# Background steps spaced by range width in a four-layer graph network

## Chip, cores and metric

The kernel runs on one core of one Trainium2 chip. The metric is the device time of a whole execution in microseconds (us), lower being better. Every engine (PE the matrix engine, PEld its weight loads, DVE the vector engine, ACT the scalar engine, POOL, and SP, which here only issues transfers) works through an instruction stream of its own, and transfers run on queues that SP, ACT and POOL issue to.

## What is computed

A network of 2708 nodes with 512 features and a sparse weighted adjacency matrix `adj` of 2708 x 2708 is run through four layers. Each adds its result to its input and normalizes the rows. Cut to what matters:

```python
deg = maximum((adj != 0).sum(-1), 1)
x = layernorm(x + L0(x, adj))   # (adj + normalized mask) @ x over row sums
x = layernorm(x + L1(x, adj))   # attention, gates, two products with adj
x = layernorm(x + L2(x, adj))   # x@w0 + A x@w1 + A A x@w2 + A A A x@w3
x = layernorm(x + L3(x, adj))   # (adj/deg-normalized @ x + x) @ W + b, relu

# in L1
s_left, s_right = h @ a_left, h @ a_right                  # h = x @ W_sa
e    = where(adj != 0, exp(-leaky_relu(s_left[:, None] + s_right[None, :])), 0)
x_a  = (e / (e.sum(1) + 1e-5)) @ h
x_b  = adj @ (x @ W_gcnb) + b_gcnb
out  = sigmoid(gate_a * x_a + gate_b * x_b)

# in L3
dinv = rsqrt(deg);  a_norm = dinv * (adj + I) * dinv
```

The counts `deg` of layer 3, one for each row of `adj`, are gathered while layer 1 runs: the sign of each element of the transposed matrix is squared (1 where it isn't zero), the squares are added up, and a matmul with ones sums over partitions.

## The kernel before

The matrix is held transposed and split into quarters (11, 12, 21, 22) of 1354 x 1354. Products with it are done in seven partial products instead of eight (P1 to P7; on PE the lines 462, 471, 480, 486, in later stages 1369), for which DVE forms combinations of quarters (s1 to s4, L407).

**Order.** The kernel is not written in the order in which it runs. Each small piece of work is put into a list with a position, `at(pos, fn)`; the list is sorted by position and the pieces are called in that order. The scheduler of the framework then orders the instructions of each engine by that order and its own estimate of times, so an instruction may be placed ahead of others that stand before it in the list. One listed as held, `at(pos, fn, True)`, may not be placed ahead of the instruction before it in the list on its own engine. A unit of position is one of the seven products of one range of columns. Stages start at the positions `S = [0, 28, 35, 91, 119, 147, 175]` and `SB = 63`.

**Stage S[1]** (position 28 to 35, one range of 330 columns) does the adjacency product of layer 1 for the columns from 1024. Beside the products, `comb` forms the sums and stores them in DRAM (SD, shown as As). `score` multiplies fetched rows of x with four vectors (L907), `scores_end` adds the halves into `s_left` and `s_right`, and `score_rows` turns columns of `s_left` into rows in DRAM: `to_rows`, a transpose on PE (L924), a copy on ACT (L926), a store by POOL (L927). `extra1` counts: `pair` has Sign twice and Square on ACT into a bf16 tile `sg` (L973, L974), and an add on DVE into `dg` (L980); `end` has the matmuls with ones (`ds`, L993) and small DVE operations, and `rows` the transpose of the reciprocals. `done1` takes the finished half results C and W through the gates (`pg`, L1018) and the dense product `ps_d` with the weights w (L610), then stores XB.

**Stage S[2]** (position 35 to 63) does the attention product of layer 1 in four ranges of seven positions each, with the columns and widths

```python
RANGES = [(0, 384), (384, 384), (768, 256), (1024, 330)]
RANGES_B = [(512, 256), (0, 256)]
```

Before a tile is used, `prep2` makes the attention weights (ACT L1156 and L1157, DVE L1158); row sums run along (L770). When a half of a range is done, DVE adds its partial results (L523: names C, W, U, P1c), at 5.05 and 7.02 positions into the range, and `done2` has the dense product with it, from 5.15 and 7.12 on.

**Background steps.** Through S[2], 22 steps run beside the product, eleven for each of two sets of 512 columns: ten full ones and a rest. A full step loads four tiles of 128 x 512, one of each quarter, in two halves (`back_load`, POOL L1067). `tally` turns two tiles into squared signs (ACT L1083, L1084) and adds them to the counts `dg` (DVE L1086), twice a step. `back_sums` forms four combinations in place (DVE L1107) and stores each (POOL L1108, As<-bk). The tiles `bk` are six in rotation: four share memory with the weights w, two with xT. `back_end` sums the counts with matmuls (L1115), and `back_rows` makes rows of them, 1.4 to 1.7 positions into the rest step. The tiles `sg` and `dg` share six slots ("nat") with fetched rows and results.

The later stages (SB, S[3] to S[6]) read the stored combinations and, in the last, the counts.

Of the kernel before, what the change touches and what calls it, by code (L numbers as in the profile page):

```python
# [24 lines left out]
ALU = mybir.AluOpType  # L25
P = 128
EPS = 1e-5
NH = 1354
KT = 11
RANGES = [(0, 384), (384, 384), (768, 256), (1024, 330)]  # L30
# [24 lines left out]
KA = 2 * KR - 32  # L55
# [16 lines left out]
def gnn_kernel(ctx: ExitStack, tc: tile.TileContext, x, adjT, w_sa, a_sa, w_gcn, b_gcn, wab, bab, w_hop, w_out,  # L72
               b_out, out):
    nc = tc.nc
# [104 lines left out]
    def at(pos, fn, hold=False):  # L179

        def go():
            n = len(nc.cur_bb.bb.instructions)
            fn()
            held.update(range(n, len(nc.cur_bb.bb.instructions)))

        events.append((pos, len(events), go if hold else fn))
# [500 lines left out]
    S = [0.0, 28.0, 35.0, 91.0, 119.0, 147.0, 175.0]  # L687
# [233 lines left out]
    def to_rows(cols, m, dst):  # L921

        ps = bank("ps_r", [P, P])
        nc.tensor.transpose(ps[:m], cols, ident)  # L924
        t = small.tile([P, P], F32, name="rows", bufs=2)
        nc.scalar.copy(t[:m], ps[:m])  # L926
        nc.gpsimd.dma_start(out=dst, in_=t[:m])  # L927

    def score_rows(R0, h, ts):
        q = slice(h * KT + ts[0], h * KT + ts[-1] + 1)  # L930
        to_rows(s_left[:, q], len(ts), SROW[R0, h])
# [13 lines left out]
    i = 0  # L945
    for R0, n in RANGES:
        full = R0 == RANGES_A[0][0]
        for h in (1, 0):
            ts = tiles_of(R0, n)
            for k in ts:  # L950
                p = S[1] + 0.55 + 0.21 * i
                at(p, lambda t=h * KT + k: get_x1(t))
                at(p + 0.25, lambda t=h * KT + k, w=wt(k), js=range(4 if full else 2): score(t, w, got1, js))
                i += 1
            at(p + 0.26, lambda a=(h * KT + ts[0], len(ts), False): scores_end(*a))
            if full:
                at(p + 0.26, lambda a=(h * KT + ts[0], len(ts), True): scores_end(*a))
            at(p + 1.5, lambda R0=R0, h=h, ts=ts: score_rows(R0, h, ts), True)
    at(p + 0.27, scores_over)
    for i, (h, k) in enumerate((h, k) for g in (4, 0) for h in (0, 1) for k in range(g, g + 4)):  # L960
        p = S[2] + 1.6 + 1.3 * i
# [5 lines left out]
    def extra1(pb, r, R0, n, A):  # L967
        ts = tiles_of(R0, n)

        def pair(keys, w=P):  # L970
            m = pool.tile([P, 2, D], BF, name="sg", tag="nat", bufs=6)
            for h, key in enumerate(keys):
                nc.scalar.activation(m[:w, h, :n], A[(r,) + key][:w, :n], AF.Sign)  # L973
            nc.scalar.activation(m[:w, :, :n], m[:w, :, :n], AF.Square)  # L974
            if R0 not in deg:
                deg[R0] = d = pool.tile([P, 2, D], BF, name="dg", tag="nat", bufs=6)
                nc.vector.tensor_copy(d[:w, :, :n], m[:w, :, :n])
            else:
                d = deg[R0]
                nc.vector.tensor_tensor(d[:w, :, :n], d[:w, :, :n], m[:w, :, :n], ALU.add)  # L980

        for k in range(KW):
            at(pb + 0.1 + 0.8 * k / KT, lambda k=k: pair((("11", k), ("21", k))), True)
            at(pb + 3.9 + 0.8 * k / KT, lambda k=k: pair((("12", k), ("22", k))), True)
        for key, w in (("r", KA), ("r32", 32)):
            at(pb + 4.8, lambda key=key, w=w: pair(((key, 0), (key, 1)), w), True)

        def end(h):
            d = deg[R0]
            ps = bank("ds", [P, 4])  # L990
            for i, q in enumerate(ts):
                wq = wt(q)
                nc.tensor.matmul(ps[:wq, i : i + 1], d[:, h, q * P - R0 : q * P - R0 + wq], ones_bf[:, 0:1], start=True,  # L993
                                 stop=True)
            for i, q in enumerate(ts):
                wq = wt(q)
                o = rdeg[:wq, h * KT + q : h * KT + q + 1]
                nc.vector.tensor_scalar(o, ps[:wq, i : i + 1], 1.0, None, ALU.max)
                nc.vector.tensor_scalar(diag[:wq, h, q : q + 1], o, 1.0, None, ALU.add)
                nc.vector.reciprocal(o, o)  # L1000

        def rows(h):
            to_rows(rdeg[:, h * KT + ts[0] : h * KT + ts[-1] + 1], len(ts),
                    DROW[h][0, ts[0] * P : (ts[-1] + 1) * P].rearrange("(k i) -> k i", i=P))

        at(pb + 5.2, lambda: end(1))
        at(pb + 5.9, lambda: rows(1))
        at(pb + 5.2, lambda: end(0))
        at(pb + 5.9, lambda: rows(0))

    def done1(p0, dp, last, R0, n, h, C, tiles):
        Z = {}
# [35 lines left out]
    back = {}  # L1048
# [13 lines left out]
    def back_load(i0, k, half):  # L1062
        if not half:
            back["next"] = {}
        for hi, hj in QUARTERS[2:] if half else QUARTERS[:2]:
            j0, c0 = hj * NH + k * P, hi * NH + i0
            nc.gpsimd.dma_start(out=back_tile((hi, hj)), in_=adjT[j0 : j0 + P, c0 : c0 + D])  # L1067
        if half:
            back["t"] = back["next"]

    def back_rest_load(i0):
        back["next"] = {}
        for h in range(2):
            a = adjT[:, h * NH + i0 : h * NH + i0 + D]
            rows_over(nc.gpsimd, back_tile((h, 0)), (a[NH - KR : NH], a[2 * NH - KR :]))
            nc.gpsimd.dma_start(out=back_tile((h, 1))[:32], in_=a[2 * NH - 32 :])
        back["t"] = back["next"]

    def tally(pair, w):

        m = pool.tile([P, 2, D], BF, name="sg", tag="nat", bufs=6)
        for h in range(2):
            nc.scalar.activation(m[:w, h, :], pair[h][:w], AF.Sign)  # L1083
        nc.scalar.activation(m[:w], m[:w], AF.Square)  # L1084
        d = back["d"][back["i0"]]
        nc.vector.tensor_tensor(d[:w], d[:w], m[:w], ALU.add)  # L1086

    def back_start(i0):
        back["i0"] = i0
        back.setdefault("d", {})[i0] = pool.tile([P, 2, D], BF, name="dg", tag="nat", bufs=6)  # L1090
        nc.gpsimd.memset(back["d"][i0], 0.0)

    def back_tally():
        t = back["t"]
        for j in range(2):
            tally([t[h, j] for h in range(2)], P)

    def back_rest_tally():
        t = back["t"]
        for j, w in ((0, KA), (1, 32)):  # L1100
            tally([t[h, j] for h in range(2)], w)

    def back_sums(i0, k):
        a21, a22, a11, a12 = (back["t"][q] for q in QUARTERS)
        for m, o, a, b, op in (("s1", a22, a21, a22, ALU.add), ("s3", a21, a11, a21, ALU.subtract),
                               ("s2", a11, a22, a11, ALU.subtract), ("s4", a12, a12, a11, ALU.subtract)):
            nc.vector.tensor_tensor(o, a, b, op)  # L1107
            nc.gpsimd.dma_start(out=SD[m][k * P : (k + 1) * P, i0 : i0 + D], in_=o)  # L1108

    def back_end(i0):  # L1110
        d = back["d"].pop(i0)
        ps = bank("ds", [P, 8])
        for h in range(2):
            for i in range(4):
                nc.tensor.matmul(ps[:, 4 * h + i : 4 * h + i + 1], d[:, h, i * P : (i + 1) * P], ones_bf[:, 0:1], start=True,  # L1115
                                 stop=True)
        for h in range(2):
            q = slice(h * KT + i0 // P, h * KT + i0 // P + 4)
            o = rdeg[:, q]
            nc.vector.tensor_scalar(o, ps[:, 4 * h : 4 * h + 4], 1.0, None, ALU.max)  # L1120
            nc.vector.tensor_scalar(diag[:, h, i0 // P : i0 // P + 4], o, 1.0, None, ALU.add)
            nc.vector.reciprocal(o, o)

    def back_rows(i0, h):
        q = h * KT + i0 // P
        to_rows(rdeg[:, q : q + 4], 4, DROW[h][0, i0 : i0 + D].rearrange("(k i) -> k i", i=P))

    p = S[2] + 1.6
    for i0, _ in RANGES_B:
        at(p, lambda i0=i0: back_start(i0))  # L1130
        for k in range(KW):
            at(p - 0.55, lambda i0=i0, k=k: back_load(i0, k, 0))
            at(p + 0.02, lambda i0=i0, k=k: back_load(i0, k, 1))
            at(p + 0.6, back_tally, True)
            at(p + 0.7, lambda i0=i0, k=k: back_sums(i0, k), True)
            p += 1.12
        at(p, lambda i0=i0: back_rest_load(i0))
        at(p + 0.6, back_rest_tally, True)
        at(p + 1.4, lambda i0=i0: back_end(i0), True)
        at(p + 1.7, lambda i0=i0: back_rows(i0, 0), True)  # L1140
        at(p + 1.72, lambda i0=i0: back_rows(i0, 1), True)
        p += 1.12

    def start2b():
        W[2] = [spare_part(s, g) for s in ("T1", "T2", "T3", "T4") for g in "BD"]
# [597 lines left out]
    for n, i in enumerate(list(nc.cur_bb.bb.instructions)):  # L1743
        p = last if n < 3 * strict else done if n in held else {}
# [44 lines left out]
```

## Time and profile before

| | |
|---|---|
| time, median of 3 runs (lowest to highest) | 2913.36 us (2912.59 to 2916.22) |
| the profiled execution: its time, its span | 2914.74 us, 2913.0 us |
| mean granted TensorE clock | 0.992 |
| S[2], first matmul to first matmul of SB | 554.2 to 1013.7 us |
| busy in S[2]: PE, DVE, ACT, POOL | 436.6, 322.9, 272.7, 124.5 us |
| a bk load of 256 KB, issue to landing (median) | 4.7 us |
| a store As<-bk of 256 KB, issue to landing (median) | 3.6 us |
| Sign, Square of the tally (median) | 614 ns, 1042 ns |
| add of the tally, combination of a step (median) | 692 ns, 686 ns |

The span runs from the first to the last recorded instruction. A line of the timeline gives start, duration, engine, line, operation, output and inputs, shape and count; a bracket at its end is the time for which the engine sat idle before it and whose event ended that. A line of waits gives the engine and line that waited, the one waited for, the total, how often, and the longest. Ends of matmuls are modelled, so a PE that is busy may still be slow: the pace of equal matmuls is what to compare.

### The profile page before, as it was taken

The page shows a single profiled execution, that of the slowest core. Times are in us where ns is not written, and L with a number is a line of the kernel's source. Part 1 is how long each engine was busy: PE and PEld are TensorE (multiplying, and loading weights), DVE is VectorE, ACT ScalarE, POOL GpSimd, SP SyncE. Part 2 cuts the span into 40 slices and gives each one's busy share as a digit, 9 for nine tenths or more (in the row PEclk, how much of TensorE's full clock was granted, in tenths as well). Part 3 has the DMA queues.
Part 4 walks back from the last instruction along what each step waited for, and adds up shares of the span by engine and source line. Part 5 has one row for each costly group of instructions (what it writes and reads, how often), then busy time and mean ns, then how long its engine had stood idle before and what let it go on. Part 6 is the DMA issues. An engine that isn't in the chain of part 4 may idle for free.

```text
span 2913.0 us, 38876 instructions
## 1 busy us (share of the span) xinstructions
PE 2824.2 (97%) x11159; PEld 1909.6 (66%) x11159; DVE 2293.2 (79%) x5890; ACT 662.2 (23%) x1314; POOL 650.6 (22%) x1175
## 2 busy tenths in 40 slices
PE   7999998999999999999999999999999999999998
PEld 5655665556676678787666666666666666656664
DVE  6989688687767667577599787887878878899986
ACT  4554204765557311202200000000000100100001
POOL 0123233212232210213203133030330212501102
PEclk9999999999999999999999999999999999999999
DMA  8666466466666565577667768566675665854642
GB/s 236 199 201 187 136 198 211 133 202 187 192 207 207 167 180 150 182 218 247 218 195 236 215 188 251 168 198 203 193 245 171 180 202 169 256 144 143 181 138 79
DMA packets 404959, 554.41 MB, mean 190 GB/s; under 512 B 68752, under 2 KB 350556, under 8 KB 404744
## 3 DMA queue, kind: packets, MB, share of 16 engines
q1 hardware_dynamic: 330976, 391.33, 45.7%
q0 software_dynamic: 56032, 148.83, 15.5%
q10 hardware_dynamic: 17736, 11.76, 1.4%
q8 instruction: 89, 1.46, 0.2%
q14 instruction: 126, 1.03, 0.1%
HBM read 468.02 MB, written 83.65 MB: 189 GB/s over the span
## 4 chain that ended last, share of the span: by engine, by line
PE 75%; DVE 10%; issue 5%; DMA 5%; POOL 2%; ACT 1%; SPq 1%; POOLq 0%; ACTq 0%; DVEq 0%
PE accd L1369 14%; PE accu L1369 13%; PE accc L1369 13%; PE ps_d L610 7%; PE acca L1369 6%; PE accu L462 4%; PE accd L462 4%; PE accr L1440 3%; PE accc L462 3%; PE acca L462 3%; DMA bk<-in_adjT 2%; DMA As<-bk 1%; DVE z L1314 1%; PE accr L1444 1%; PE ps L649 1%
## 5 line engine op out<-in xcount | busy, mean ns | idle before, releaser
L1314 DVE TENSOR_TENSOR z<-z 128x339 f32<-128x339 f32 (+2 forms) x1176 | 538.4, 490 | 19.9 <-PE accu L1369 10.6
L1387 ACT COPY q<-accu 128x339 f32<-128x339 f32 (+2 forms) x105 | 41.7, 429 | 1057.7 <-PE accu L1369 907.7
L1369 PE MATMUL accc<-s,t 128*128 128x339 f32 (+2 forms) x784 | 233.5, 439 | 0.2 <-DVE s L1314 0.2
L1369 PE MATMUL accu<-z,t 128*128 128x339 f32 (+2 forms) x784 | 227.7, 436 | 4.2 <-DVE z L1314 3.0
L1369 PE MATMUL accd<-z,t 128*128 128x339 f32 (+2 forms) x784 | 227.8, 436 | 2.2 <-DVE q L1451 1.4
L1369 PE MATMUL accc<-z,t 128*128 128x339 f32 (+2 forms) x784 | 226.8, 436 | 0.5 <-ACT q L1387 0.5
L564 POOL TENSOR_TENSOR rstd<-rstd,neg_half 128x1 f32<-128x1 f32 (+3 forms) x91 | 60.2, 662 | 710.0 <-DVE rstd L563 454.5
L1369 PEld LDWEIGHTS accu<-z,t 128*128 128x128 f32 x784 | 148.1, 190 | 70.1 <-DVE z L1314 6.1
L1369 PEld LDWEIGHTS accc<-s,t 128*128 128x128 f32 x784 | 146.8, 190 | 70.7 <-issue 10.2
L1369 PEld LDWEIGHTS accd<-z,t 128*128 128x128 f32 x784 | 148.1, 190 | 67.2 <-DVE q L1451 2.3
L1369 PEld LDWEIGHTS accc<-z,t 128*128 128x128 f32 x784 | 148.2, 190 | 64.8 <-ACT q L1387 1.0
L1393 DVE TENSOR_TENSOR q<-q,accd 128x338 f32<-128x338 f32 (+2 forms) x140 | 67.9, 485 | 148.7 <-PE accd L1369 148.3
L1314 DVE TENSOR_TENSOR s<-z 128x339 f32<-128x339 f32 (+2 forms) x392 | 178.1, 489 | 7.2 <-PE accc L1369 3.1
L1588 POOL DMA_DIRECT2D Y<-y x192 | 104.8, 552 | 327.0 <-DVE y L1583 289.8
L407 DVE TENSOR_TENSOR a<-a,a 128x384 f32<-128x384 f32 (+2 forms) x240 | 118.5, 514 | 7.1 <-ACT sg L973 6.1
L1158 DVE SCALAR_TENSOR_TENSOR a<-a,e 128x384 f32<-128x384 f32 (+2 forms) x160 | 78.4, 507 | 36.2 <-ACT e L1157 34.7
L1156 ACT ACTIVATE e<-row,s_right 128x384 f32<-128x384 f32 (+5 forms) x176 | 95.4, 566 | 37.6 <-DVE a L1158 17.9
L569 ACT ACTIVATE ld<-ld,rstd 128x512 f32<-128x512 f32 (+3 forms) x45 | 36.5, 813 | 263.9 <-DVE rstd L566 98.4
L1451 DVE TENSOR_TENSOR q<-q,accr 128x338 f32<-128x338 f32 (+2 forms) x160 | 69.1, 484 | 22.8 <-PE accr L1444 22.7
L1393 DVE TENSOR_TENSOR q<-q,accu 128x338 f32<-128x338 f32 (+2 forms) x175 | 79.2, 485 | 3.9 <-ACT q L1387 2.7
L1157 ACT ACTIVATE e<-e 128x384 f32<-128x384 f32 (+5 forms) x176 | 80.0, 476 | 1.7
L774 DVE SCALAR_TENSOR_TENSOR s<-a,row 128x384 f32<-128x384 f32 (+2 forms) x152 | 75.3, 508 | 6.0 <-ACT row L759 6.0
(699 smaller groups left out, 5897.6 us busy)
## 6 DMA issues: line engine op xcount, KB each, us to landing
z<-As SPq DMA_DIRECT2D x320, 169.5 KB
z<-As SPq DMA_DIRECT2D x320, 169.0 KB
z<-in_adjT SPq DMA_DIRECT2D x240, 169.5 KB
z<-in_adjT SPq DMA_DIRECT2D x240, 169.0 KB
a<-in_adjT SPq DMA_DIRECT2D x160, 192.0 KB
bk<-in_adjT POOLq DMA_DIRECT2D x80, 256.0 KB, 4.7
As<-bk POOLq DMA_DIRECT2D x80, 256.0 KB, 3.6
z<-As SPq DMA_DIRECT2D x160, 128.0 KB
```

Of the source, the lines that this page charges most:

```text
L407: nc.vector.tensor_tensor(A[r, dst, k][:, :n], A[r, a, k][:, :n], A[r, b, k][:, :n], op)
L462: nc.tensor.matmul(B[home, c][:, :n], X[STAT[p], k][:, c * P : (c + 1) * P], A[r, MOV[p], k][:, :n], start=bool(start and k == k0), stop=k ...
L610: nc.tensor.matmul(o, lhs(c), r, start=c == 0 and n == 0, stop=c == DC - 1, skip_group_check=True)
L774: nc.vector.scalar_tensor_tensor(t[:w, :n], a[:w, :n], 0.0, row[R0, h][:w, :n], ALU.is_gt, ALU.mult)
L1156: nc.scalar.activation(e[:w, :n], row[R0, h][:w, :n], AF.Prelu, bias=s_right[:w, t : t + 1], alpha=0.01)
L1157: nc.scalar.activation(e[:w, :n], e[:w, :n], AF.Exp, scale=-1.0)
L1158: nc.vector.scalar_tensor_tensor(a[:w, :n], a[:w, :n], 0.0, e[:w, :n], ALU.not_equal, ALU.mult)
L1314: nc.vector.tensor_tensor(d[:, :n], Z[x + (k,)][:, :n], Z[y + (k,)][:, :n], op)
L1369: nc.tensor.matmul(B[home][:, :n], stat(v, k), a[:, :n], start=bool(start and k == 0), stop=k == nk - 1, skip_group_check=True)
L1393: nc.vector.tensor_tensor(d[:, :n], s_[:, :n], B[home][:, :n], ALU.add)
L1440: nc.tensor.matmul(ps[r][:, :n], XA[:KA, c * P : (c + 1) * P], R[h, s][:KA, :n], start=True, stop=False, skip_group_check=True)
L1588: nc.gpsimd.dma_start(out=rows[:, :, f * P : (f + 1) * P], in_=o[32 * f : 32 * (f + 1), : m * P].rearrange("p (b d) -> p b d", d=P))
```

## The change

Three groups of edits; no operation of the arithmetic is added, dropped or changed.

1. The background steps get positions from a time scale. A range of n columns counts as n + 60 per position, `place_at` turns a time on that scale into a position, and 22 steps lie at equal distances `dt`. Before, a step took 1.12 positions in every range.
2. `pair` and `tally` only square, and the add is a piece of its own (`add`, `back_add`), listed later: 0.1 position in S[1], 0.08 of a step in S[2]. A step's two tallies are listed apart, too. The squares of the rests in S[1] go from 4.8 to 5.0.
3. `score_rows` is listed at 4.5 (columns from 0) or 6.2 positions into S[1], where each stood 1.5 after its last tile's fetch. In S[1] `end` goes from 5.2 to 7.0 and `rows` from 5.9 to 7.5, both held now.

```diff
-            at(p + 1.5, lambda R0=R0, h=h, ts=ts: score_rows(R0, h, ts), True)
+            at(S[1] + (6.2 if R0 else 4.5) + 0.01 * i, lambda R0=R0, h=h, ts=ts: score_rows(R0, h, ts), True)
...
             nc.scalar.activation(m[:w, :, :n], m[:w, :, :n], AF.Square)
+            ms.append((m, w))
+
+        def add():
+            m, w = ms.pop(0)
             if R0 not in deg:
...
             at(pb + 0.1 + 0.8 * k / KT, lambda k=k: pair((("11", k), ("21", k))), True)
+            at(pb + 0.2 + 0.8 * k / KT, add, True)
             at(pb + 3.9 + 0.8 * k / KT, lambda k=k: pair((("12", k), ("22", k))), True)
+            at(pb + 4.0 + 0.8 * k / KT, add, True)
         for key, w in (("r", KA), ("r32", 32)):
-            at(pb + 4.8, lambda key=key, w=w: pair(((key, 0), (key, 1)), w), True)
+            at(pb + 5.0, lambda key=key, w=w: pair(((key, 0), (key, 1)), w), True)
+            at(pb + 5.0, add, True)
...
-        at(pb + 5.2, lambda: end(1))
-        at(pb + 5.9, lambda: rows(1))
-        at(pb + 5.2, lambda: end(0))
-        at(pb + 5.9, lambda: rows(0))
+        for h in (1, 0):
+            at(pb + 7.0, lambda h=h: end(h), True)
+            at(pb + 7.5, lambda h=h: rows(h), True)
...
         nc.scalar.activation(m[:w], m[:w], AF.Square)
+        back["m"].append((m, w))
+
+    def back_add():
         d = back["d"][back["i0"]]
-        nc.vector.tensor_tensor(d[:w], d[:w], m[:w], ALU.add)
+        for m, w in back["m"]:
+            nc.vector.tensor_tensor(d[:w], d[:w], m[:w], ALU.add)
+        back["m"].clear()
...
-    p = S[2] + 1.6
+    widths = [n + 60 for _, n in RANGES]
+    ends = [7 * sum(widths[:i]) for i in range(5)]
+
+    def place_at(t):
+
+        i = max(i for i in range(4) if ends[i] <= t)
+        return S[2] + 7 * i + (t - ends[i]) / widths[i]
+
+    t0, dt = 1.0 * widths[0], (26.4 / 28 * ends[4] - widths[0]) / 21
+    at_t = lambda j, fn, hold=False: at(place_at(t0 + dt * j), fn, hold)
+    j = 0
     for i0, _ in RANGES_B:
-        at(p, lambda i0=i0: back_start(i0))
+        at_t(j, lambda i0=i0: back_start(i0))
         for k in range(KW):
-            at(p - 0.55, lambda i0=i0, k=k: back_load(i0, k, 0))
-            at(p + 0.02, lambda i0=i0, k=k: back_load(i0, k, 1))
-            at(p + 0.6, back_tally, True)
-            at(p + 0.7, lambda i0=i0, k=k: back_sums(i0, k), True)
-            p += 1.12
-        at(p, lambda i0=i0: back_rest_load(i0))
-        at(p + 0.6, back_rest_tally, True)
-        at(p + 1.4, lambda i0=i0: back_end(i0), True)
-        at(p + 1.7, lambda i0=i0: back_rows(i0, 0), True)
-        at(p + 1.72, lambda i0=i0: back_rows(i0, 1), True)
-        p += 1.12
+            at_t(j - 0.5, lambda i0=i0, k=k: back_load(i0, k, 0))
+            at_t(j + 0.02, lambda i0=i0, k=k: back_load(i0, k, 1))
+            for e in range(2):
+                at_t(j + 0.5 + 0.08 * e, lambda e=e: back_tally(e), True)
+                at_t(j + 0.58 + 0.08 * e, back_add, True)
+            at_t(j + 0.67, lambda i0=i0, k=k: back_sums(i0, k), True)
+            j += 1
+        at_t(j, lambda i0=i0: back_rest_load(i0))
+        for e in range(2):
+            at_t(j + 0.5 + 0.08 * e, lambda e=e: back_rest_tally(e), True)
+            at_t(j + 0.58 + 0.08 * e, back_add, True)
+        at_t(j + 1.3, lambda i0=i0: back_end(i0), True)
+        at_t(j + 1.6, lambda i0=i0: back_rows(i0, 0), True)
+        at_t(j + 1.62, lambda i0=i0: back_rows(i0, 1), True)
+        j += 1
```

More of the change, by code (lines that the diff above doesn't have):

```diff
@@ L968, in extra1 @@
         ts = tiles_of(R0, n)
+        ms = []
         def pair(keys, w=P):
@@ L1084, in tally, with back_tally, back_rest_tally @@
         nc.scalar.activation(m[:w], m[:w], AF.Square)
+        back["m"].append((m, w))
+    def back_add():
         d = back["d"][back["i0"]]
-        nc.vector.tensor_tensor(d[:w], d[:w], m[:w], ALU.add)
+        for m, w in back["m"]:
+            nc.vector.tensor_tensor(d[:w], d[:w], m[:w], ALU.add)
+        back["m"].clear()
     def back_start(i0):
         back["i0"] = i0
+        back["m"] = []
         back.setdefault("d", {})[i0] = pool.tile([P, 2, D], BF, name="dg", tag="nat", bufs=6)
         nc.gpsimd.memset(back["d"][i0], 0.0)
-    def back_tally():
+    def back_tally(j):
         t = back["t"]
-        for j in range(2):
-            tally([t[h, j] for h in range(2)], P)
-    def back_rest_tally():
+        tally([t[h, j] for h in range(2)], P)
+    def back_rest_tally(j):
         t = back["t"]
-        for j, w in ((0, KA), (1, 32)):
-            tally([t[h, j] for h in range(2)], w)
+        tally([t[h, j] for h in range(2)], (KA, 32)[j])
     def back_sums(i0, k):
```

## The prediction

> **What bounds the kernel now.** I read the page's first parts, then busy time by stretch, then the PE timeline for its gaps, then what the engines behind each gap waited for. The page's busy table and its chain of work:
>
> ```profile
> PE 2824.2 (97%) x11159; PEld 1909.6 (66%) x11159; DVE 2293.2 (79%) x5890; ACT 662.2 (23%) x1314; POOL 650.6 (22%) x1175
> ...
> PE 75%; DVE 10%; issue 5%; DMA 5%; POOL 2%; ACT 1%; SPq 1%; POOLq 0%; ACTq 0%; DVEq 0%
> ```
>
> PE is the bound, so a change that leaves the matmuls alone, as this one does, can save only PE gaps and the slow matmuls after them. It touches the end of S[1] and S[2]. I split S[2] at the first matmul of each range (554.2, 678.3, 800.2, 894.2, end 1013.7 us). Columns: stretch; its length; busy PE, PEld, DVE, ACT, POOL; clock; DMA share; GB/s.
>
> ```profile
> 554.20:678.30 124.10, 121.27 (x411) 71.92 (x410) 92.24 (x216) 84.43 (x152) 26.94 (x49) 1.00 0.60 181
> 678.30:800.20 121.90, 119.97 (x422) 76.23 (x421) 83.30 (x215) 70.44 (x137) 32.50 (x60) 1.00 0.61 189
> 800.20:894.20 94.00, 86.79 (x411) 74.27 (x410) 60.65 (x173) 55.89 (x114) 29.34 (x55) 0.96 0.65 207
> 894.20:1013.70 119.50, 108.58 (x428) 76.33 (x426) 86.74 (x227) 61.95 (x120) 35.76 (x65) 0.96 0.60 186
> ```
>
> No other engine is full. PE idles 22.9 us in all, 18 of them in the last two stretches. In the PE timeline it is five gaps (bracket: idle before, and releaser), each at the end of a range where the dense product takes a finished half result (C or P1c, an add of L523):
>
> ```profile
> 640.34 0.70 PE L610 MATMUL ps_d<-T1B,C 128*128 128x256 f32 x2 [2.83 <-DVE C L523]
> 762.17 0.70 PE L610 MATMUL ps_d<-T1B,C 128*128 128x256 f32 x2 [1.93 <-DVE C L523]
> 867.01 1.22 PE L610 MATMUL ps_d<-T1B,C 128*128 128x256 f32 x2 [7.07 <-DVE C L523]
> 902.48 1.19 PE L610 MATMUL ps_d<-T1B,P1c 128*128 128x256 f32 x2 [5.89 <-DVE P1c L523]
> 975.34 1.22 PE L610 MATMUL ps_d<-T1B,C 128*128 128x256 f32 x2 [5.03 <-DVE C L523]
> ```
>
> The matmuls after the three long gaps are slow: the same 16 matmuls of 256 columns take 3.45 us in the chain at 769.76 but 5.62 (867.01 to 872.63), 5.10 (902.48) and 6.22 us (975.34), so 2.17 + 1.65 + 2.77 us more, and 0.27 us after each short gap. The gaps cost S[2] 22.75 + 7.13 = **29.9 us**.
>
> What made DVE late, from the waits of the stretch of S[2] (total us, times, longest):
>
> ```profile
> ACT sg L1083 <- DMA bk<-in_adjT: 65.9, 15, 12.8
> POOL bk L1067 <- DMA As<-bk: 59.1, 36, 4.3
> DVE dg L1086 <- ACT sg L1084: 58.9, 18, 15.2
> ```
>
> This is the background work in a ring of six bk tiles: a load waits for an earlier store, Sign waits for the load, the add of the counts waits for Square, and everything behind that add on DVE waits too. A step that is behind restarts after about 15.5 us (Sign of successive steps at 813.11, 828.56, 843.92, 855.25, 873.14, 888.66). Its list asks for one each 1.12 positions: 19.7 us in ranges 0 and 1 (1.12/7 x 123), **15.0 us in range 2**, 19.1 in range 3. Range 2 asks for more than the ring gives, and there the backlog and the long gaps start.
>
> S[1] ends otherwise. Two PE gaps, both by list order:
>
> ```profile
> 474.23 0.27 PE L924 MATMUL ps_r<-ident,s_left 128*3 128x128 f32 x1 [4.36 <-DVE s_left L918]
> 521.20 0.40 PE L993 MATMUL ds<-ones_bf,dg 128*128 128x1 bf16 x6 [6.29 <-DVE dg L980]
> 518.68 0.49 DVE L523 TENSOR_TENSOR W<-W,accu 128x330 f32<-128x330 f32 x1
> ```
>
> DVE is nearly full there (24.3 of the 25 us from 497 to 522). The last operand of the gate matmuls, W, is written at 519.1.
>
> **What the Trainium skill says.** "TensorE: Matmul & The Clock Gate", Part 1, What's actually happening: after an idle window of about 3.4 us the array runs at half rate, until about 3.4 us of work. The trace agrees: slow matmuls follow the gaps of 5 to 7 us, hardly those of 1.9 and 2.8. "PSUM — Partial Sum Buffer", Engine vs sequencer instructions: the queues of ScalarE, VectorE and GpSimdE are strict FIFO. Agreed: DVE stood 15.16 us before one add at 700.77. "DMA: Bandwidth & Descriptors", Anatomy of one DMA — SWDGE path: 2.0 us plus bytes/436e3, an estimate of 2.6 us for 256 KB. The trace has 4.7 us for a bk load and 3.6 for a store; I use those.
>
> **The change, part by part.** No arithmetic is added or removed. All 22 steps keep 4 loads and 4 stores (bar the two rests), 6 ACT instructions (4 x 0.62 + 2 x 1.04 = 4.6 us), and on DVE 2 adds (0.69) and 4 combinations (0.69), 4.1 us. Only places move.
>
> *Spacing.* With widths 444, 444, 316, 390 and 7 positions each, dt is 479.8, so a step is 1.08 positions in ranges 0 and 1, 1.52 in range 2, 1.23 in range 3. Times the measured lengths that is 19.2, 18.8, 20.4 and 21.0 us: above the ring's 15.5 everywhere. Tallies that fall in each range go from 5, 6, 6, 5 to 6, 6, 5, 5. On POOL the loads and stores move with the step, past stores of XB only; the first loads can't start before 571.6, when the last product with w ends and frees their tiles. By gap:
> - 867: step 15 was listed at 19.0 to 19.1, on top of C (19.05); now 19.27 to 19.53, behind it. Ahead of C vanish 4.1 us of DVE work, waits of 1.21 and 0.42, and the 3.39 us at 846. That is 9.1 against 7.07: gap 0.5 us left, no slow matmuls.
> - 902: P1c is listed at 21.02. Step 16's combinations go from 20.22 to 21.04 and its second add to 21.03: 3.4 us of DVE work falls behind P1c. 5.89 - 3.4 = 2.5, plus 0.3 slow.
> - 975: the rest goes from 25.72 to 26.98, behind C (26.05), and takes 1.37 us of adds and waits of 1.35 and 1.43 along. But step 20 comes to 25.75 to 25.96, with its own 4.1 us. About even: 4.0 plus 1.5.
> - 640: step 3 comes to 4.78 to 4.97, right ahead of C (5.05), where step 2 stood at 4.44. It starts earlier too, so I take a gap of 4.0 plus 0.3, one us more.
> - 762: step 9 at 11.27 to 11.45 for step 8 at 11.16 to 11.26, 3 us later, C at 12.05: 2.5 plus 0.3.
>
> Sum 15.9 us for 29.9: **14.0 saved**.
>
> *Adds after squares.* In S[2] an add now stands 0.08 of a step (1.5 us) after its tally, less than the 2.3 us of Sign, Sign, Square; it hides some of the short waits, none of the long ones, and these are counted above. Each sg tile lives a little longer in the six nat slots; sg and its add still alternate, so I take 0, from -2 to +2. In S[1] the adds didn't wait for Square at all (the trace lists no idle time of L980), so 0 too; the sg tiles there live about one us longer beside the fetched rows. The squares of the rests go from 4.8 to 5.0, with their adds; W (5.06) stays behind them in the list, though the trace has the adds after W (519.89, 520.65), so 0.
>
> *Score rows and sums later.* The first score rows leave 2.5 for 4.5, so the 474 gap (4.36 + 1.69 of slow matmuls) goes, and ds leaves 5.2 for 7.0. But the next thing that PE asks of DVE is W at 519.1, and DVE does the same work up to it. PE only arrives earlier and waits longer. What is left is 521.2 + 0.33 (the ds matmuls) - 519.1 = 2.4, less 0.4 for a longer cold start: **2.0 saved**. Bounds: -14.7 if PE finds other matmuls to do (both gaps with their slow matmuls), +5 if dg, now held until 7.0, leaves y too few nat slots. The rows are due by 5.4 for the row load; 0.85 positions (some 9 us) cover transpose 0.27, copy 0.25 and store 2.2.
>
> *Tail.* Last sums at 27.96, rows at 28.34: PE waits there for adds listed 0.8 positions (12 us) earlier. If that cover is gone, one gap of some 5 us.
>
> Sum -16.0. The profiled execution took 2914.74 us (span 2913.0), 1.38 above the median of 2913.36. 2914.74 - 16.0 - 1.38 = **2897.4**.
>
> **Rivals.** *A: nearly all gaps close* (adds reach DVE in time): four fifths of 29.9, plus 6 of S[1], is -30: 2883. For it: PE is covered wherever DVE isn't late. Against: three blocks now stand right before a result that PE wants. *B: nothing measurable*, 2913: DVE owes the same work at the same results, and gaps only move between ranges. Against: DVE was idle 59 us before adds. *C: slower.* Steps 3, 16 and 20 now stand on the results at 5.05, 21.02 and 26.05. If Square ends later than the result's last matmul, DVE stands at the held add, with the combinations after it, and C comes behind both: up to 4.6 + 2.75 = 7.4 us, plus 2 of cold matmuls. Three of those are 28.2 against 18.4 at these places now, and if 867 keeps its gap nothing pays for it: +9.8, 2923. It decides once ACT is more than some 3 us behind at those places, as it was in 8 of the 18 waits. *D: the steps aren't equally far apart on the chip*, since the scheduler orders engines by its own estimate: gains half as large, 2905.
>
> **How the numbers follow.** About 0.2%, 5.8 us, is what a measurement of this kernel can tell from no change. Main forecast 0.38, A 0.12, D 0.10, B 0.12, C 0.28. Of the three gaining cases (0.60) I put 0.01 within the bound and 0.02 beyond it: faster 0.57, same 0.13, slower 0.30. Range 2879 to 2925: A with most of S[1]'s bound below, C with 2 us of slots above. The faster cases' own range is 2879 to 2907.
>
> **What would show it.** Right: no gap over 2 us at the C of range 2, no wait of Sign for bk over 6 us there, range 2 at 85 to 88 us, the wait of dg for Square under 40 us in all, no PE wait on s_left at 474, the gate matmuls waiting for W instead. Wrong: range 0 longer than 127 us, a wait of over 7 us before the products of ranges 0 or 3, or PE waiting on y or nat slots from 522 to 554. Any gain outside 405 to 1014 us would be another cause.

## The result, and the profile after

The changed kernel took 2931.84 us (median; 2928.94 to 2936.07) against 2913.84 for the kernel before, timed beside it: a ratio of 1.0062, 95% interval 1.0044 to 1.0079, so **18 us slower**, with 2897 forecast. Run again later, in a group of its own, it came to 1.0041 (1.0026 to 1.0057), 12 us slower. The first part of its page and the head of its chain of work:

```profile
PE 2835.4 (97%) x11159; PEld 1919.3 (65%) x11159; DVE 2296.9 (78%) x5890; ACT 660.9 (23%) x1313; POOL 651.9 (22%) x1175
...
PE 76%; DVE 10%; DMA 6%; issue 3%; ACT 2%; POOL 1%; SPq 1%; DVEq 0%; POOLq 0%; ACTq 0%
```

Nothing shows here: every engine has the work of before, and PE is still the bound. The busy times by range (the same columns as before, split at the first matmul of each range) show where it went:

```profile
552.20:685.66 133.46, 123.43 (x417) 73.56 (x415) 97.89 (x239) 91.03 (x166) 33.93 (x63) 0.96 0.59 183
685.66:811.21 125.55, 121.59 (x430) 77.57 (x429) 87.10 (x225) 69.94 (x139) 34.63 (x64) 0.99 0.58 174
811.21:904.23 93.02, 89.12 (x403) 76.00 (x403) 58.29 (x171) 52.15 (x112) 25.79 (x49) 0.94 0.64 206
904.23:1021.27 117.04, 105.89 (x397) 74.35 (x396) 81.09 (x193) 59.82 (x110) 27.80 (x51) 0.94 0.57 170
```

Range 0 went from 124.1 to 133.5 us with 10 us of idle PE in it, range 1 from 121.9 to 125.6, and ranges 2 and 3 together gained only 3.4. The PE timeline has these gaps now, the first in S[1]:

```profile
515.46 2.07 PE L1026 MATMUL pg<-C,wab_pad 128*32 128x330 f32 x4 [6.35 <-DVE C L523]
645.85 1.22 PE L610 MATMUL ps_d<-T1B,C 128*128 128x256 f32 x2 [10.03 <-DVE C L523]
771.58 0.70 PE L610 MATMUL ps_d<-T1B,C 128*128 128x256 f32 x2 [3.96 <-DVE C L523]
872.18 0.98 PE L783 MATMUL rs<-ones_f,run 128*128 128x1 f32 x4 [3.38 <-DVE run L770]
877.30 1.19 PE L610 MATMUL ps_d<-T1B,C 128*128 128x256 f32 x2 [0.52 <-DVE rd L1195]
910.39 1.19 PE L610 MATMUL ps_d<-T1B,P1c 128*128 128x256 f32 x2 [3.83 <-ACT e L1182]
984.30 1.22 PE L610 MATMUL ps_d<-T1B,C 128*128 128x256 f32 x2 [4.78 <-DVE C L523]
1017.79 0.68 PE L599 MATMUL ps_t<-ident,ld 128*128 128x128 f32 x4 [2.54 <-ACT ld L569]
1029.67 0.48 PE L599 MATMUL ps_t<-ident,ld 74*128 74x74 f32 x4 [2.40 <-ACT ld L569]
```

In S[1] both gaps of before are gone, and PE waits for C at the gates. The 7.07 us at C of range 2 has become a wait for row sums, the 2.83 of range 0 has become 10.03, and the last two lines are new: transposes of normalized rows around the start of SB, which PE never waited for before.

The surest measure is the lag: the start of a matmul of the product, changed kernel minus kernel before, the same matmul by count. (The profiled executions took 2934.22 and 2914.74 us; the other run of the changed kernel 2937.13.)

| up to | before, us | lag | lag, run again |
|---|---|---|---|
| S[1], ahead of the score rows | 469.4 | +3.6 | +5.0 |
| S[1], after them | 489.7 | -2.8 | -1.4 |
| range 0, ahead of C | 637.0 | -1.7 | +0.5 |
| range 0, after C | 669.6 | +7.4 | +11.6 |
| range 1, after C | 784.2 | +11.1 | +16.6 |
| range 2, after C | 896.1 | +10.0 | +16.0 |
| range 2, after P1c | 919.5 | +9.2 | +12.4 |
| range 3, after C | 1003.9 | +7.6 | +11.7 |
| SB | 1044.9 | +17.7 | +21.6 |
| last product | 2809.0 | +19.4 | +22.4 |

Two places lose some 10 us each, C of range 0 and the end of S[2], and C of range 1 loses some 4; S[1] gains 6.4 at the score rows. The totals of the ring's waits in S[2] didn't move (before: 65.9, 59.1 and 58.9):

```profile
ACT sg L1091 <- DMA bk<-in_adjT: 66.3, 16, 12.3
POOL bk L1075 <- DMA As<-bk: 62.4, 40, 4.0
DVE dg L1098 <- ACT sg L1092: 59.5, 26, 16.9
```

### The profile page after: what moved, and what is told of

It reads as the page before. It is cut to its first block, busy times and chain, and to the rows that moved or that the text cites. A ratio compares the mean times of both kernels' runs of the same rounds, so it can differ in the third digit from the quotient of the medians.

```text
span 2932.4 us, 38866 instructions
## 1 busy us (share of the span) xinstructions
PE 2835.4 (97%) x11159; PEld 1919.3 (65%) x11159; DVE 2296.9 (78%) x5890; ACT 660.9 (23%) x1313; POOL 651.9 (22%) x1175
## 4 chain that ended last, share of the span: by engine, by line
PE 76%; DVE 10%; DMA 6%; issue 3%; ACT 2%; POOL 1%; SPq 1%; DVEq 0%; POOLq 0%; ACTq 0%
PE accd L1395 13%; PE accu L1395 13%; PE accc L1395 13%; PE ps_d L610 7%; PE acca L1395 6%; PE accu L462 5%; PE accd L462 4%; PE accc L462 4%; PE accr L1466 3%; PE acca L462 3%; DMA bk<-in_adjT 1%; DVE z L1340 1%; PE accr L1470 1%; PE ps L649 1%; DVE vy L907 1%
```

## The experiments

Eleven runs, each timed beside the kernel before on its chip. There the kernel before had medians of 2918 to 2920 us, so the absolute figures in the expectations, which start from 2914, are to be read against that; I use ratios. Lags by place are of one execution each. In e3, e7 and e8 below, whose S[2] is that of the kernel before, the lag still changes by up to 3.4 us at C of range 0 and by up to 2.4 at the other places, but by less than 0.1 from range 3 to SB. A change by place of under about 3 us is therefore not told from none, unless several runs repeat it.

**The change in three parts.** e1, spacing alone, each add in one piece with its square:

```diff
-        back["m"].append((m, w))
+        d = back["d"][back["i0"]]
+        nc.vector.tensor_tensor(d[:w], d[:w], m[:w], ALU.add)
...
-                at_t(j + 0.58 + 0.08 * e, back_add, True)
```

(Diffs in this part are against the changed kernel, unless another is named. Here S[1] is that of the kernel before, too.)

> Only the new time scale of the background steps in S[2]; every add stays in one piece with its square, and S[1] is as before. Theory 1 (the places do it: step 3 and step 9 now stand on DVE right ahead of C of ranges 0 and 1, and the rest step comes behind U in range 3): the whole loss is here, 2926 to 2934 us against 2914, with a gap of 8 to 10 us before the products with C of range 0, about 4 at range 1, under 1 at range 2 (867), and SB starting some 10 us later than C of range 3 explains. Theory 2 (the split of square and add does it, by longer use of the nat slots): within 4 us of the kernel before, or faster by up to 10, since the gaps of range 2 close and no slot is held longer.

Measured: 1.0002 (0.9992 to 1.0011), no difference. The gap in range 0 is there (10.36 us, a lag of 10.3 from that place), and 4.0 more are lost at P1c of range 0; but ranges 2 and 3 pay for it, with 3.9 us at C of range 2, 4.2 at P1c and 8.1 at C of range 3. The end of S[2] loses only 1.5. Theory 1 had the place right and the total wrong. Theory 2 had the total right, but not the whole of its reason: the gaps of range 2 did shrink, and range 0 paid for it.

e2, the split alone, with the old places:

```diff
-        i = max(i for i in range(4) if ends[i] <= t)
-        return S[2] + 7 * i + (t - ends[i]) / widths[i]
+        return S[2] + t
...
-    t0, dt = 1.0 * widths[0], (26.4 / 28 * ends[4] - widths[0]) / 21
+    t0, dt = 1.6, 1.12
```

> Only the split of tally and add in S[2] with the adds 0.08 of a step later; the steps keep 1.12 positions in every range, S[1] is as before. Theory 1 (the places do it): within 3 us of the kernel before (2911 to 2917), no gap over 4 us before C of range 0, the five gaps of before still there. Theory 2 (slots held by squares whose add comes later): 2922 to 2930, with fetches of X rows on SP that wait for an add into dg, and late transposes ps_t before SB.

Measured: 0.9996 (0.9987 to 1.0005). Later adds alone cost nothing, and the gaps of before are there (9.67 at C of range 2, 6.28 at range 3), but for that at C of range 0, which is gone.

e3, the edits of S[1] alone (against the kernel before; the adds as in the change):

```diff
-            at(p + 1.5, lambda R0=R0, h=h, ts=ts: score_rows(R0, h, ts), True)
+            at(S[1] + (6.2 if R0 else 4.5) + 0.01 * i, lambda R0=R0, h=h, ts=ts: score_rows(R0, h, ts), True)
...
+            at(pb + 7.0, lambda h=h: end(h), True)
+            at(pb + 7.5, lambda h=h: rows(h), True)
```

> Only the edits of S[1]: counts added later, score rows at 4.5 and 6.2, sums at 7.0, their rows at 7.5; S[2] is as before. Theory 1: 2 us faster (2910 to 2914); the PE gap before the transposes of s_left (474) is gone, the products with the gates wait for C or W some 4 to 6 us instead, and the loss of 3.7 us at 461 seen in the changed kernel (a matrix load on ACT's queue behind the store of X) does not come back, being a matter of that execution. Rival: the loss at 461 belongs to the edits, and the kernel is 1 to 4 us slower than before.

Measured: 0.9974 (0.9963 to 0.9986), **7.5 us faster**, not 2. The 3.6 us that the changed kernel had lost ahead of the score rows didn't come back. Some 3 us are lost there in some executions (e5 2.7 with the edits, e10 3.0 without) and under 0.4 in others (e3, e4, e6), so they aren't the edits'.

So three parts of +0.5, -1.4 and -7.5 us make +12 to +18 together. Something exists only in the combination. The two next runs look for it.

e10, spacing and split together, with the S[1] of the kernel before:

```diff
-            at(S[1] + (6.2 if R0 else 4.5) + 0.01 * i, lambda R0=R0, h=h, ts=ts: score_rows(R0, h, ts), True)
+            at(p + 1.5, lambda R0=R0, h=h, ts=ts: score_rows(R0, h, ts), True)
...
-            at(pb + 7.0, lambda h=h: end(h), True)
+        at(pb + 5.2, lambda: end(1))
```

> The changed kernel with S[1] as it was before: spacing and split of S[2] together, without the edits of S[1]. Theory (the two need each other to do harm, S[1] has no part in it): the changed kernel's loss plus the 7.5 us that the edits of S[1] save, so 17 to 24 us slower than the kernel before, 9 to 11 of it between C of range 3 and SB. Rival (it is the S[1] edits that set S[2] off badly, since PE reaches it earlier): within 6 us of the kernel before.

Measured: 1.0052 (1.0032 to 1.0072), 15 us slower, less than the 17 to 24 of the theory but far from the rival. S[1] has no part in the loss. The loss at C of range 0 was 7.9 us and the one between range 3 and SB 8.3. Its PE timeline shows both:

```profile
647.42 1.22 PE L610 MATMUL ps_d<-T1B,C 128*128 128x256 f32 x2 [9.29 <-DVE C L523]
...
1021.95 0.47 PE L599 MATMUL ps_t<-ident,ld 74*128 74x74 f32 x4 [2.79 <-ACT ld L569]
```

**The end of S[2].** In the changed kernel the chain there reads, in the order of time (timelines of DVE and SP):

```profile
1008.45 0.91 DVE L523 TENSOR_TENSOR U<-U,accd 128x330 f32<-128x330 f32 x2 [2.58 <-PE accd L486]
1009.27 0.69 DVE L1098 TENSOR_TENSOR dg<-dg,sg 116x1024 bf16<-116x1024 bf16 x1
1009.98 0.32 SPq L152 DMA_DIRECT2D ld<-X  x1
1014.16 0.69 DVE L1207 TENSOR_TENSOR ld<-ld 128x512 f32<-128x512 f32 x1 [2.88 <-DMA ld<-X]
```

The rest step was squared on ACT at 989.5, but its add stands on DVE behind U, which waits for PE. At 1009.96 the add ends, and 0.02 us later SP issues the fetch of an X row, into the nat slot that the squares had held. The row is added at 1014.16, normalized, and transposed late. Before, that fetch left at 972.79. To test it, e4 lets the rest steps use no nat slot, at the same places in the list:

```diff
-        t = back["t"]
-        tally([t[h, j] for h in range(2)], (KA, 32)[j])
+        t, w = back["t"], (KA, 32)[j]
+        for h in range(2): nc.scalar.activation(t[h, j][:w], t[h, j][:w], AF.Sign); nc.scalar.activation(t[h, j][:w], t[h, j][:w], AF.Square); back["m"].append((h, t[h, j], w))
```

> The changed kernel, but the two rest steps take Sign and Square in place in their own bk tiles and add from there, in four adds of 512 instead of two of 1024; they use no nat slot, and their places in the list are the same. If the late end of S[2] comes from the slots that the rest step's squares hold until their adds behind U (theory 1 for the tail): about 10 us faster than the changed kernel, 2920 to 2924, the fetches of the X rows of range 3 leave SP before 990 us instead of at 1010, and PE has no gap over 1 us before ps_t between 1010 and 1055. If the adds behind U themselves are what is late (rival: DVE's order), at most 3 us of the 10 come back: 2928 to 2932.

Measured: 1.0017 (1.001 to 1.0023), 5 us slower than the kernel before, so 7 to 13 better than the changed kernel. The adds run as late as ever, after U, and yet the fetches leave early (SP of e4):

```profile
972.76 4.71 SPq L152 DMA_DIRECT2D ld<-X  x2
```

The lag from range 3 to SB is 0.6 us instead of 10. This is the slot, not DVE's order. e1 confirms it: there the rest's add stands ahead of U, and frees the slot 10 us sooner (DVE and SP of e1):

```profile
998.75 0.68 DVE L1086 TENSOR_TENSOR dg<-dg,sg 116x1024 bf16<-116x1024 bf16 x1
999.45 0.32 SPq L152 DMA_DIRECT2D ld<-X  x1
```

In e2 the rest step comes at about the time of C, as before (adds at 977.3 and 979.5, C from 978.0), and its late adds free the slots in time. Harm takes both: a rest step so late that its add falls behind U, which the spacing brings near and the split completes.

**C of range 3.** The end of S[2] is only one of two places that tell e10 from e1, which differ in the split alone: e10 loses 8.3 us there for 1.5. The other is C of range 3, where e1 gains 8.1 us and e9 (below, also in one piece) 7.9, while e10, the changed kernel in both executions and e4 gain 0.2 to 1.7, with step 20 listed ahead of C in all of them. The traces show a difference in the order on DVE. Step 19 in e1, then in the changed kernel run again:

```profile
960.59 0.68 DVE L1112 TENSOR_TENSOR bk<-bk 128x512 f32<-128x512 f32 x1
962.21 0.68 DVE L1086 TENSOR_TENSOR dg<-dg,sg 128x1024 bf16<-128x1024 bf16 x1
```

```profile
965.63 0.69 DVE L1098 TENSOR_TENSOR dg<-dg,sg 128x1024 bf16<-128x1024 bf16 x1 [0.82 <-ACT sg L1092]
966.24 0.69 DVE L1119 TENSOR_TENSOR bk<-bk 128x512 f32<-128x512 f32 x1
```

In one piece, two of the step's combinations run before its second add; split, all four come behind it. Their stores leave later, and so do the loads that wait for the stores: Sign of step 20 begins 13.1 us after that of step 19 in e1, 15.7 in the changed kernel run again (13.0 in e9, 15.4 in e10). So the split also slows the ring. That this is why C of range 3 keeps its gap is read from the order; no run tests it alone.

**C of range 0.** In the changed kernel (ACT, then DVE):

```profile
639.64 1.15 ACT L1091 ACTIVATE sg<-bk 128x512 bf16<-128x512 f32 x2 [12.32 <-DMA bk<-in_adjT]
641.91 0.69 DVE L1098 TENSOR_TENSOR dg<-dg,sg 128x1024 bf16<-128x1024 bf16 x1 [3.88 <-ACT sg L1092]
644.04 0.69 DVE L1098 TENSOR_TENSOR dg<-dg,sg 128x1024 bf16<-128x1024 bf16 x1 [1.44 <-ACT sg L1092]
644.65 0.69 DVE L1119 TENSOR_TENSOR bk<-bk 128x512 f32<-128x512 f32 x1
645.25 0.55 DVE L523 TENSOR_TENSOR C<-U,accc 128x384 f32<-128x384 f32 x1
```

DVE is free at 638.03 and stands before step 3's adds for 3.88 and 1.44 us, because Sign came late, because its loads landed late; C comes behind. e5 moves only step 3 behind C:

```diff
-    at_t = lambda j, fn, hold=False: at(place_at(t0 + dt * j), fn, hold)
+    at_t = lambda j, fn, hold=False: at(place_at(t0 + dt * (j + 0.45 * (hold and 3.4 < j < 3.7) + 0.12 * (4.01 < j < 4.03))), fn, hold)
```

> The changed kernel with step 3 alone moved: its squares, adds and combinations come 0.45 of a step later, 5.27 to 5.46 positions into range 0 and so behind C (5.05), and one half of step 4's loads 0.12 of a step later. Theory 1 (a held block right ahead of C makes C late): the gap of 10 us before the products with C of range 0 shrinks to at most 2 us, 8 to 11 us less than the changed kernel. Rival (the ring is behind by itself in range 0, so that C, or what follows it, waits all the same): the gap moves to the next product that DVE feeds in range 0 or 1, and at most 4 us are saved.

The changed kernel itself ran in the same group:

> The changed kernel once more, on the chip and between the runs with which the others of this group are compared. If spacing and split add up (theory: sum of the parts, +0.5, -1.4 and -7.5 us), it is some 8 us faster than the kernel before. If the two need each other to do harm (theory: a late rest step whose squares wait for late adds keeps two nat slots), it is 15 to 22 us slower, and the loss between C of range 3 and the first product of SB is 9 to 11 us again.

Measured: the changed kernel 1.0041 (1.0026 to 1.0057), e5 1.0009 (1.0000 to 1.0017), so 9.4 us better. The gap is now 3.71 us (range 0's C of e5, behind the row sums and scores that DVE has in front of it):

```profile
641.24 1.22 PE L610 MATMUL ps_d<-T1B,C 128*128 128x256 f32 x2 [3.71 <-DVE C L523]
```

It isn't the 2 us of theory 1, but e3, e7 and e8, where no step was moved, have 3.0 to 3.4 there. And nothing moved on to range 1 as the rival had it: the lag at C of range 1 grows by 1.5 instead of 5.0.

**All causes away.** e6 has e4's counting in place, e5's step 3, and step 20 behind C of range 3:

```diff
+    at_t = lambda j, fn, hold=False: at(place_at(t0 + dt * (j + 0.45 * (hold and 3.4 < j < 3.7) + 0.12 * (4.01 < j < 4.03) + 0.32 * (hold and 20.4 < j < 20.7))), fn, hold)
```

> The changed kernel with the three causes taken away together: the rest steps count in place (no nat slot), step 3 behind C of range 0, and step 20's squares, adds and combinations 0.32 of a step later, 26.15 to 26.35 and so behind C of range 3 (26.05). Theory 1: against the run without slots (+4 us to the kernel before) 10 us less at range 0 and 5 to 7 less at range 3, so 11 to 14 us faster than the kernel before and faster than the S[1] edits alone (7.5 us). Rival (what is moved behind C comes back at U and P1c, listed 0.95 positions later): no more than 4 us faster than the kernel before.

Measured: 0.9964 (0.9953 to 0.9975), **10.5 us faster than the kernel before**. That is just short of theory 1. C of range 3 has no gap left and gains 8.3 us; the lag at SB is -6.7. Against the 7.5 us of e3, the edits of S[1] alone, the 3 us more aren't clear of the intervals: even mended, the new places of S[2] are not shown to gain anything.

e9 keeps adds and squares in one piece in S[2] (e1's diff), with e5's step 3 (e5's diff) and the S[1] of the change:

> The changed kernel, but in S[2] every add stays in one piece with its square, and step 3's squares, adds and combinations are 0.45 of a step later, behind C of range 0 (one half of step 4's loads 0.12 later). If the parts add up: spacing +0.5, S[1] -7.5, step 3 -9.4, so 13 to 18 us faster than the kernel before, with no late transposes before SB. Rival (spacing needs the split in range 2, and without it the gaps of range 2 come back): 4 to 9 us faster.

Measured: 0.9968 (0.9954 to 0.9981), 9.3 us faster, short of the 13 to 18. What is missing lies at P1c of range 0, where this kernel loses 6.7 us. DVE of e9:

```profile
676.28 0.69 DVE L1094 TENSOR_TENSOR dg<-dg,sg 128x1024 bf16<-128x1024 bf16 x1 [4.64 <-ACT sg L1092]
677.42 2.86 DVE L1120 TENSOR_TENSOR bk<-bk 128x512 f32<-128x512 f32 x4
680.20 0.55 DVE L523 TENSOR_TENSOR P1c<-P1c,acca 128x384 f32<-128x384 f32 x1
```

Step 5 is listed at 6.94 to 7.13, across P1c at 7.02. In one piece its first add and its combinations stand ahead of P1c, and the add waits for Square; split, as in the changed kernel, they come behind P1c (685.26, then the adds at 686.76), and nothing is lost. Here the split lets a result pass.

**S[1] in parts.** Against the kernel before, e7 takes the first two lines of e3's diff alone, the score rows; e8 the last two alone, the sums and their rows:

> The kernel before with one edit: score_rows at 4.5 (columns from 0) and 6.2 positions into S[1]; adds, sums and their rows as before. Theory 1 (the S[1] gain is the transposes' gap at 474, and the sums' place matters too, since dg and the scores before it stood ahead of W on DVE): 474 closes, but the sums still wait at 521 for dg by as much as PE comes earlier, so at most 2 us faster. Rival (the rows alone carry the gain of S[1]): 5 to 8 us faster.

> The kernel before with one edit of S[1]: sums at 7.0 and their rows at 7.5 positions, held; score rows and adds as before. Theory (the gains of S[1] need both: the rows' gap at 474 closes only if the rows move, the wait at 521 only if the sums move): the gap at 474 stays at 4 to 5 us, the wait at 521 goes over to the products with the gates, and the kernel is 0 to 4 us faster. Rival (the sums alone carry it): 5 to 8 us faster.

Measured: e7 0.9993 (0.9987 to 1.0000), at most 4 us faster and 2 by the middle; e8 1.0001 (0.9990 to 1.0012), nothing. Together with the later adds, which no run has alone, they are e3's 7.5. PE of e7, of e8 (two lines) and of e3:

```profile
522.81 0.40 PE L993 MATMUL ds<-ones_bf,dg 128*128 128x1 bf16 x6 [12.82 <-DVE dg L980]
```

```profile
473.80 0.37 PE L924 MATMUL ps_r<-ident,s_left 128*3 128x128 f32 x1 [4.07 <-DVE s_left L918]
516.29 1.31 PE L1018 MATMUL pg<-C,wab_pad 128*32 128x330 f32 x2 [3.21 <-DVE C L523]
```

```profile
511.62 2.06 PE L1026 MATMUL pg<-C,wab_pad 128*32 128x330 f32 x4 [7.95 <-DVE C L523]
```

In e7 PE reaches the sums early and waits there 12.82 us; in e8 the gap at the rows stays, and the wait at the gates is short. With both, and the later adds, PE comes early to the gates and goes on at 511.6, where before it stood at the sums until 521.2.

## Why the prediction was wrong

**S[1]: right that the gap goes, wrong on what bounds it.** The step "DVE does the same work up to W" failed. W was written at 519.1 before; in e3 the second W starts at 513.34. From 440 us on, 82 score operations (L907) stand ahead of that W in e3 and 94 in the kernel before; four adds into dg come behind it (two of them at 516.43 and 517.52), where it was two. In e7 and e8 the counts are those of before, so it takes the two edits together or the later adds; which of them isn't known. The 2.0 was mis-sized: 6.4 us at the rows, 7.5 in all, within the bound of 14.7 that I had set.

**640 is the first failed step of S[2].** "It starts earlier too, so I take a gap of 4.0": an earlier place in the list isn't an equally earlier start. The first loads, listed at 0.46 positions where it was 1.05, so some 10 us earlier, leave at 572.5 instead of 574.2, and the ring of stores and loads then sets the pace. Step 3 takes the place of step 2 ahead of C, 0.34 positions (6 us) later in the list, but its Sign began at 639.6 where that of step 2 had begun at 628.6, and PE was out of work at 635.8. The gap was 10.03, and the place cost 9.05 us with its slow matmuls, for 1.2 forecast (a gap of 4.0 for one of 2.83). This is rival C at its own price: 7.2 us of C's delay (10.03 - 2.83) where it said up to 7.4, and 1.85 of slow matmuls where it said 2. I gave it 0.28 and three places; e5 shows it for range 0.

**762**: 3.96 for a forecast of 2.5, with 3.7 us lost there and not 0.6: 1.7 us of slow matmuls came with it, which I had priced at 0.3.

**867 is the second failed step: the work to be taken away was another step's.** "Ahead of C vanish 4.1 us of DVE work, waits of 1.21 and 0.42, and the 3.39 us at 846" was said of step 15. But the rest of the first set is step 10, and its last Sign, of 32 rows, stands at 784.23, so the Signs at 813.11, 828.56, 843.92 and 855.25 are those of steps 11 to 14, and the one at 873.14 is step 15's (ACT, kernel before):

```profile
784.23 1.13 ACT L1083 ACTIVATE sg<-bk 32x512 bf16<-32x512 f32 x2
873.14 1.15 ACT L1083 ACTIVATE sg<-bk 128x512 bf16<-128x512 f32 x2 [12.77 <-DMA bk<-in_adjT]
```

On the chip step 15 was behind C (866.54) already. The waits of 1.21 and 0.42 are step 14's and that of 3.39 is step 13's. Step 14 was listed at 17.88 to 17.98 and is now at 17.75 to 18.01: the change takes nothing away ahead of C. In the changed kernel step 14's combinations still stand there (866.20 to 869.70), with the row sums behind them; PE now waits 3.38 us for `run` and is slow afterwards. 8.7 us of gain were forecast, 0.6 came, and between -0.4 and 1.8 in the five other runs with the split. In e1 and e9, with the adds in one piece, 3.9 and 4.2 came. Why the split takes those 3 us is open.

**902** went to 3.83, now a wait for ACT, for 2.5 forecast: 0.8 us gained in one execution, 3.6 in the other, for 4.7. **975** was right, 4.78 for 4.0, with 1.7 us gained for 2.3 (0.8 when run again). The sum for slow matmuls was a little high: at four gaps they were read to the end of the last matmul and set against 3.45 us read to the next start, 0.16 us too much each.

**Adds later: "0, from -2 to +2" is the third failed step.** I named the six nat slots, and asked only whether squares and adds still alternate. I didn't ask for how long the last square holds its slot once its add falls behind U, or who waits for that slot: the fetch of X, the normalization, the transposes of SB. It cost 8 to 10 us. The tail in the prediction looked at the sums at 27.96 alone. Nor did I ask whether the combinations still go ahead of the second add; with the split they don't, and the ring's step ahead of C of range 3 took 15.7 us where e1 and e9 have some 13.

**The ring.** Waits of Square were to fall under 40 us; they stayed at 59.5. Even distances in the list didn't make even ones on the chip: the first Signs of steps 2 to 6 began at 621.0, 639.6, 666.7, 680.0 and 709.5, so 13 to 30 us apart for a listed 19. That is what rival D said; what equal steps would have been worth isn't tested.

By the terms, from the table: S[2] up to its end +9.3 (its five places 9.7) for -14.0 forecast, the end +10.1 for 0, and S[1] from the score rows on -5.3 for -2.0; the +3.6 ahead of them aren't the edits'. "Range 0 longer than 127 us" (133.5) and "a wait of over 7 us before the products of range 0" (10.03) were the signs that I named for being wrong.

## What to carry to other kernels

Before you move a step in a list, follow three things: which result is listed right behind it on the same engine and whether its inputs can be there by then; which buffer it holds until its last reader and what is queued for that buffer; and what the bound engine asks for next when the gap is gone. Parts of a change that are harmless alone (+0.5 and -1.4 us here) can cost 15 us together. About half of it here came from one part that moves a reader behind a wait and another that makes the buffer live until that reader; the other half lies at C of range 3, where the split takes away what the spacing gains. A split of a producer and its held reader pays where it lets a result pass between them, and costs where the reader then falls behind a result that comes late.

## What the runs showed that I had not expected

The release of a tile carries to another engine almost at once: the fetch of X was issued 0.02 us after the add's end in the changed kernel and in e1. The slow matmuls can set in after PE has gone on. After the gap of 3.96 us the first two pairs ran at full pace, and the slow ones followed (PE timeline of the changed kernel):

```profile
772.11 0.63 PE L610 MATMUL ps_d<-T1D,C 128*128 128x256 f32 x2
772.54 1.06 PE L610 MATMUL ps_d<-T2B,C 128*128 128x256 f32 x2
...
775.10 1.02 PE L610 MATMUL ps_d<-T3D,W 128*128 128x256 f32 x2
775.95 0.60 PE L610 MATMUL ps_d<-T4B,W 128*128 128x256 f32 x2
```

The eight pairs took 5.24 us to the next start, 776.82, where they took 3.55 before.

The prediction took a limit of some 3.4 us from the Trainium skill's page "TensorE: Matmul & The Clock Gate", Part 1, What's actually happening. In these runs, before products with C or P1c in S[2], gaps of 3.78 us and more all had slow matmuls behind them, and gaps of up to 1.95 us that stand alone had none. Between these the length didn't decide: a gap of 3.56 us in e9 had none behind it, one of 2.99 us in e8 had four slow pairs (the second pair of each):

```profile
899.45 0.67 PE L610 MATMUL ps_d<-T1B,P1c 128*128 128x256 f32 x2 [3.56 <-ACT e L1181]
899.95 0.59 PE L610 MATMUL ps_d<-T1D,P1c 128*128 128x256 f32 x2
```

```profile
638.88 1.03 PE L610 MATMUL ps_d<-T1B,C 128*128 128x256 f32 x2 [2.99 <-DVE C L523]
639.70 1.06 PE L610 MATMUL ps_d<-T1D,C 128*128 128x256 f32 x2
```

So a gap of 2 to 3.8 us cost 0 to 3.1 us beside its own length (3.1 after 3.71 us in e5), and its length didn't tell which.

An add of 512 elements with one 4-byte operand isn't cheaper by half than one of 1024 in bf16: four of them took 2.48 us in e4, 0.62 each, for 0.69.
